# Who converts the gather indices: ScalarE ahead of time, or GpSimd in the place of a pause

## The chip, the cores and the metric

One core of a Trainium2 chip runs the whole program in one launch. The metric is the time of an execution on the device in microseconds (us); the kernel before has a median of 3063.61 us over three runs (3060.14 to 3072.32).

Five engines work beside each other, each in the order of its own program: TensorE (PE in the profile, with its weight loads as PEld), VectorE (DVE), ScalarE (ACT), GpSimd (POOL) and the queue of SyncE (SP), which here only issues transfers. They wait for each other by semaphores.

## The reference

A graph with 6250 nodes of 128 features and 200,000 edges, sorted by destination, goes through a layer norm with a ReLU and three layers of a GraphSAGE convolution. The output is the input plus the last layer's result.

```python
def _sage_conv(x, src, dst, Wl, bl, Wr):
    agg = jax.ops.segment_max(x[src], dst, num_segments=x.shape[0])
    agg = jnp.where(jnp.isfinite(agg), agg, 0.0)
    return agg @ Wl + bl + x @ Wr
...
h = jax.nn.leaky_relu(_sage_conv(h, src, dst, Wl, bl, Wr), 0.01)   # three times: 128 -> 256 -> 256 -> 128
```

What takes the time is `segment_max(x[src], dst)`: for each node the maximum, feature by feature, over the rows of all its neighbours. The neighbours are drawn at random, and some nodes have many more than others.

## The kernel before

Nodes stand in 50 tiles of up to 127. The kernel finds each node's maximum in two ways at once, and splits its edges between them.

The first way uses TensorE. Source nodes are taken two tiles at a time, in 25 pairs. For each pair, and for each block of destination nodes, an index says which source row (at most one in each half of the pair) the destination takes. ScalarE turns the indices into a one-hot matrix (`hot`, L1014 and L1016), TensorE multiplies the pair's features with it (L1033, into the PSUM tile `pg`, three buffers), and VectorE takes the maximum into `acc` (L1057). One such block is a step; the whole program is written out by hand as a row of steps over three layers.

The second way is for the edges that remain, and the change is in it. They stand in five lists (`Listed`, one object for each list and layer). A list has rows `q` of length `CAPS[k][q]`; each element of a row is one gather: GpSimd reads 128 indices, one for each partition, and issues an indirect DMA that fetches 128 rows of the layer's table from DRAM into a slot of the tile `g` (L1095). A layer has 503 gathers, the program 1509. Four gathers (eight in the first layer, whose rows are half as wide) fill one tile `g`, and there are 8 such tiles. When a tile is full, VectorE takes its maximum with the row's first tile (`maximum`, L1113), and at the row's end folds the slots together (`fold`, L1135); the result goes to DRAM (`store`), from where each node tile fetches it later (L1174).

The indices lie in SBUF as 16-bit numbers (`ell`, and `deep` for the first few gathers of a list), and the gather wants 32-bit ones. So up to four columns at a time (fewer at the end of a row) are converted into a small tile `let`, of which there are 14. `release` does that with a ScalarE activation (L1084). It is called for every gather, returns at once unless the gather is the first of its four, and stands in the program two steps ahead of that gather (`LEAD`).

Behind each gather stands a pause (L1102): GpSimd writes a tile of 128 x 300 that nobody reads. The pause is left out for the two gathers that follow a GpSimd subtraction in the second and third layer (`paused`, `SPARE`, L944); 1355 pauses are written in all.

`plan(t, rank, f)` puts a piece of work into step `t`; the ranks order the pieces within the step. At L1420 to L1423 each gather gets a step (`whens`, spread evenly over the layer), its `release` an earlier one and its `maximum` a later one (`delay`: 4 to 8 steps). GpSimd, like the others, works through its pieces in the order in which they were planned. Beside the gathers it has the fetches of L1174 and L1245, the subtractions of L944 for finished node tiles in the second and third layer, and, in the first layer, the scatters of L660 that build the lists; a small write of 128 x 1 stands ahead of each of those (L659).

Of the kernel before, what the change touches and what calls it, by code (L numbers as in the profile page):

```python
# [39 lines left out]
AF = mybir.ActivationFunctionType  # L40
# [31 lines left out]
FIRST = 24  # L72
# [5 lines left out]
def kernel(ctx: ExitStack, tc: tile.TileContext, x, src, dst,  # L78
                    Wl1, bl1, Wr1, Wl2, bl2, Wr2, Wl3, bl3, Wr3, out):
    nc = tc.nc  # L80
# [835 lines left out]
    for (f, k), s in best.items():  # L916
        n = len(LISTS[k]) * P
# [20 lines left out]
    paused = [0]  # L938
# [121 lines left out]
    class Listed:  # L1060
# [14 lines left out]

        def release(self, t):
            q, j = self.seq[t]
            if j % self.n:
                return
            assert here_now[0] >= listed_at[self.k]  # L1080
            n = min(self.n, self.long(q) - j)
            self.lets[q, j // self.n] = let = ring.tile([P, 4], I32, tag="let", name="let", bufs=14)
            of = ell[self.k][:, q, j : j + n] if q >= 0 else deep[self.k][:, j : j + n]
            nc.scalar.activation(let[:, :n], of, AF.Identity, scale=1.0)  # L1084

        def gather(self, t):
            q, j = self.seq[t]
            b, i = divmod(j, self.B)
            if i == 0:
                self.tiles[q, b] = ring.tile([P, self.B, self.F], F32, tag="g", name="g", bufs=RING)  # L1090
            if j % self.n == self.n - 1 or j == self.long(q) - 1:
                let = self.lets.pop((q, j // self.n))
            else:
                let = self.lets[q, j // self.n]
            nc.gpsimd.indirect_dma_start(  # L1095
                out=self.tiles[q, b][:, i, :], out_offset=None, in_=tables[self.layer],
                in_offset=bass.IndirectOffsetOnAxis(ap=let[:, j % self.n : j % self.n + 1], axis=0),
            )
            if paused[0]:
                paused[0] -= 1  # L1100
            else:
                nc.gpsimd.memset(gap_t, 0.0)  # L1102
# [184 lines left out]
    for layer in range(3):  # L1287
        begins.append(len(steps))
        for n in range(max(STARTS[layer]) + NG):
# [3 lines left out]
            of = {}  # L1293
# [16 lines left out]
    def plan(t, rank, f):  # L1310
        agenda.setdefault((t, rank), []).append(f)

    LET, TURN, MAXIMA, ROWS, REST, LINEAR, MERGE, SOONER, GATHER, FETCH = range(10)
    LEAD = 2
# [64 lines left out]
    def delay(layer, t):  # L1379
        return DELAY[layer] - (0 if layer else 4 if t < 92 else 2 if t < 150 else 0)  # L1380

    def heavy(layer, t):
        if layer:
            return WIDER if steps[t][3][3] is not None else 1.0
        return next((1.0 + w for w, until in zip(SLOWER, (58, 92, 150)) if t < until), 1.0)
# [17 lines left out]
    for layer in range(3):  # L1403
        b0, end = begins[layer], begins[layer + 1]
        lists_ = [Listed(layer, k) for k in range(NL)]
        whens = []
        for part, t0, t1 in ((lists_, max(b0 + 2, rows_at) if layer else EARLY, end - 1 - SOON),):
            total = [0.0]
            for t in range(t0, t1):
                total.append(total[-1] + heavy(layer, t))  # L1410
            n = sum(len(li.seq) for li in part)
            t = 0
            for i in range(n):
                while total[t + 1] <= total[-1] * i / n:
                    t += 1
                whens.append(t0 + t)
        done_at, i, at = [], 0, 0
        for k, li in enumerate(lists_):
            for t in range(len(li.seq)):
                plan(max(whens[i] - LEAD, 0) if layer or k or t >= FIRST else 0, LET, lambda li=li, t=t: li.release(t))  # L1420
                plan(whens[i], GATHER, lambda li=li, t=t: li.gather(t))
                at = max(at, whens[i] + (SOON if k == NL - 1 else delay(layer, whens[i])))
                plan(at, MAXIMA, lambda li=li, t=t: li.maximum(t))  # L1423
                last = t == len(li.seq) - 1
                to = at
                for n, f in enumerate(li.folds(t)):
                    if f == li.beside or n == 0 or (n and not last and li.seq[t][0] != 0):
                        to += 1
                    plan(to, MAXIMA, f)
                i += 1  # L1430
            done_at.append(to)
        gap = (2, 3, 3)[layer]
        def begin(key, make):
            def f():
                accs[key] = make()
                accs[key].fetch()
            return f

        def stages(ta, key, make, after=(3, 4, 5, 6)):
            plan(ta, FETCH, begin(key, make))  # L1440
            for d, rank, stage in (
                (after[0], MERGE, "merge"), (after[1], LINEAR, "linear"),
                (after[2], ROWS if after[2] > after[1] else SOONER, "rows"), (after[3], TURN, "turn"), (after[3], REST, "rest"),
            ):
                plan(ta + d, rank, lambda stage=stage: getattr(accs[key], stage)())

        def ready(k, i):
            return max(ends_at[layer, k], done_at[LISTED[GROUPS[k][i]][0]] + gap) + 1

        def node_of(k, i):  # L1450
            return (layer, k, "node", i), lambda layer=layer: Node(layer, k, i, accs[layer, k])

        joins = ready(VIRT, 0)
        key = (layer, "joined")

        def start(key=key, layer=layer):
            accs[key] = Joined(layer, accs[layer, VIRT])

        plan(joins, MAXIMA, start)
        for v in range(NV):  # L1460
            plan(joins + v, FETCH, lambda key=key, v=v: accs[key].fetch(v))
            plan(joins + 2 + v, MERGE, lambda key=key, v=v: accs[key].merge(v))
        for i in range(widths[layer] // P):
            plan(joins + 10, MERGE, lambda key=key, i=i: accs[key].scan(i))
        for v in range(NV):
            plan(joins + 11 + v, TURN, lambda key=key, v=v: accs[key].send(v))
        virtual_at = joins + 11 + NV + 2
        t, waiting = 0, [(layer, None, a) for a in range(VT)]
        for k, every in ((0, 1 if layer == 0 else 2), (1, 1 if layer == 0 else 2), (3, 1)):
            for i in range(len(GROUPS[k]) - 1, -1, -1):  # L1470
                t = max(t, ready(k, i))
                while waiting and t >= virtual_at:
                    a = waiting[0][2]
                    stages(t, waiting.pop(0), lambda layer=layer, a=a: Node(layer, None, a, None))
                    t += every
                stages(t, *node_of(k, i))
                t += every
        assert not waiting
        t0 = max(t, end, done_at[-1] + 1) + 1
        for j, i in enumerate(range(len(GROUPS[4]) - 1, -1, -1)):  # L1480
            stages(t0, *node_of(4, i), after=[d + j for d in (2, 3, 3, 4)])
        rows_at = t0 + 3 + len(GROUPS[4]) - 1
# [31 lines left out]
    for t in range(max(max(agenda)[0] + 1, len(steps) + 1)):  # L1514
# [10 lines left out]
        if t < len(steps):  # L1525
            st = steps[t]
            layer, k, _, _, _ = st
            if (layer, k) not in accs:
                i, o = ACC[k]
# [21 lines left out]
        def pair_at(t):  # L1551
            return steps[t][0], steps[t][4], steps[t][2]

        if here and (t == 0 or pair_at(t - 1) != pair_at(t)):
            i = at_pair[pair_at(t)] + 2
# [288 lines left out]
```

## Time and profile before

| | us |
|---|---|
| median of three runs | 3063.61 |
| the profiled execution | 3057.92 |
| its span, first to last instruction | 3056.0 |

The span has four parts: about 240 us in which the index tables are made, and then the three layers, whose gathers run from 241 to 1161, from 1224 to 2088 and from 2152 to 3005 us. In the second and third layer the first 450 us or so hold the list gathers with little else on GpSimd; after that the node tiles are finished beside the remaining gathers.

How to read the rows further down: a group of instructions has its line in the kernel, its engine, what it writes and reads (out<-in), the count behind an x, then busy time in us and the mean of one in ns. "Idle before" is the time in which the engine stood still right before these instructions, and the name behind the arrow is what ended most of it. In a timeline the same stands in brackets. "Issue" is time in which the engine waited for nothing that the profile shows.

### The profile page before, as it was taken

The page shows a single profiled execution, that of the slowest core. Times are in us where ns is not written, and L with a number is a line of the kernel's source. Part 1 is how long each engine was busy: PE and PEld are TensorE (multiplying, and loading weights), DVE is VectorE, ACT ScalarE, POOL GpSimd, SP SyncE. Part 2 cuts the span into 40 slices and gives each one's busy share as a digit, 9 for nine tenths or more (in the row PEclk, how much of TensorE's full clock was granted, in tenths as well). Part 3 has the DMA queues.
Part 4 walks back from the last instruction along what each step waited for, and adds up shares of the span by engine and source line. Part 5 has one row for each costly group of instructions (what it writes and reads, how often), then busy time and mean ns, then how long its engine had stood idle before and what let it go on. Part 6 is the DMA issues. An engine that isn't in the chain of part 4 may idle for free. (4 is left out here: it accounts for less than half of the span.)

```text
span 3056.0 us, 37265 instructions
## 1 busy us (share of the span) xinstructions
PE 2253.3 (74%) x9371; PEld 1679.8 (55%) x9371; DVE 2464.3 (81%) x4113; ACT 1551.2 (51%) x2734; POOL 2435.0 (80%) x3346
## 2 busy tenths in 40 slices
PE   1013545356665777998888879999899888878887
PEld 1012433344443545776666667776676666657665
DVE  6587966977896975898898988885798899988885
ACT  5204569466843766555455435555555545444342
POOL 6746888878888883888888887884788888887784
PEclk9996777677877999999999999999999999999998
DMA  9404434347754787555454547787555544546675
GB/s 257 130 6 129 125 98 120 105 122 226 225 156 150 226 243 254 163 167 180 134 162 152 160 148 237 248 265 263 160 170 164 159 138 151 173 148 183 196 220 161
DMA packets 301988, 525.13 MB, mean 172 GB/s; under 512 B 56769, under 2 KB 164439, under 8 KB 301125
## 3 DMA queue, kind: packets, MB, share of 16 engines
q1 hardware_dynamic: 205679, 293.70, 29.8%
q0 software_dynamic: 78016, 194.75, 23.2%
q10 hardware_dynamic: 18070, 34.20, 3.0%
q8 instruction: 79, 1.29, 0.2%
q14 instruction: 144, 1.18, 0.1%
HBM read 399.93 MB, written 122.51 MB: 171 GB/s over the span
## 5 line engine op out<-in xcount | busy, mean ns | idle before, releaser
L1033 PE MATMUL pg<-hot,pair_sb 128*128 128x512 f32 (+2 forms) x7500 | 1965.3, 411 | 422.0 <-DVE acc L1057 194.7
L1033 PEld LDWEIGHTS pg<-hot,pair_sb 128*128 128x128 f32 x7500 | 1412.4, 201 | 842.0 <-issue 291.4
L1095 POOL DMA_INDIRECT g<-table,let x1509 | 1531.1, 1015 | 346.0 <-issue 253.4
L1057 DVE TENSOR_TENSOR acc<-acc,pg 128x1024 f32<-128x1024 f32 (+5 forms) x1539 | 1543.2, 1024 | 238.5 <-PE pg L1033 130.8
L1016 ACT ACTIVATE hot<-idx_sb 128x1024 fp32r<-128x1024 uint8 (+3 forms) x975 | 839.5, 881 | 679.5 <-PE pg L1033 448.5
L1102 POOL MEMSET gap_t<- 128x300 f32 x1355 | 506.9, 374 | 0.6
L1014 ACT ACTIVATE hot<-idx_sb,last_b 128x1024 fp32r<-128x1024 int8 (+2 forms) x375 | 355.9, 949 | 33.8 <-PE pg L1033 24.7
L1113 DVE TENSOR_TENSOR g<-g 128x1024 f32<-128x1024 f32 (+7 forms) x211 | 209.6, 993 | 30.6 <-DMA g<-table,let 29.5
L1209 ACT ACTIVATE s<-z_p 127x256 f32<-127x256 f32 (+1 forms) x150 | 52.1, 347 | 329.0 <-PE z_p L1205 146.8
L1174 POOL DMA_INDIRECT agg<-best,end_i x141 | 142.5, 1011 | 54.2 <-PE aT_p L1190 22.7
L1135 DVE TENSOR_TENSOR g<-g 128x256 f32<-128x256 f32 (+2 forms) x365 | 174.8, 484 | 10.9 <-issue 6.5
L1203 PE MATMUL z_p<-wr,hT_in 128*128 128x256 f32 (+1 forms) x500 | 135.1, 387 | 0.7 <-DMA hT_in<-across 0.7
L1205 PE MATMUL z_p<-wl,mz 128*128 128x256 f32 (+1 forms) x500 | 121.0, 359 | 9.9 <-DVE mz L1196 7.7
L1004 DVE TENSOR_SCALAR idx_sb<-idx_sb,own_b 128x512 int32<-128x512 int32 (+4 forms) x125 | 74.3, 595 | 43.8 <-DMA idx_sb<-idx 35.5
L1203 PEld LDWEIGHTS z_p<-wr,hT_in 128*128 128x128 f32 x500 | 78.7, 199 | 42.4 <-issue 25.7
L1205 PEld LDWEIGHTS z_p<-wl,mz 128*128 128x128 f32 x500 | 88.4, 202 | 22.6 <-DVE mz L1196 10.2
L660 POOL DMA_INDIRECT picks<-picked,to_i x52 | 55.8, 1074 | 55.0 <-DVE rank_h L636 28.9
L1196 DVE TENSOR_TENSOR mz<-acc,aT_p 128x256 f32<-128x256 f32 (+1 forms) x141 | 52.1, 370 | 57.1 <-PE aT_p L1190 41.9
L793 DVE TENSOR_TENSOR acc<-acc 128x1300 int16<-128x1300 int16 (+6 forms) x120 | 62.2, 518 | 41.9 <-issue 20.0
L828 ACT CAST v<-lk_p 25x1024 uint8<-25x1024 bf16 (+4 forms) x15 | 10.8, 737 | 148.3 <-PE lk_p L826 134.7
L944 POOL TENSOR_TENSOR h<-s,h 127x256 f32<-127x256 f32 x50 | 37.9, 758 | 58.3 <-ACT h L1210 54.0
L1190 PE MATMUL aT_p<-ident,agg 128*128 128x128 f32 x250 | 57.1, 295 | 29.7 <-DMA agg<-best,end_i 17.1
(303 smaller groups left out, 1362.2 us busy)
## 6 DMA issues: line engine op xcount, KB each, us to landing
pair_sb<-pair SPq DMA_DIRECT2D x106, 512.0 KB
pair<-pr SPq DMA_DIRECT2D x100, 256.0 KB
g<-table,let POOLq DMA_INDIRECT x1509
pair_sb<-pair SPq DMA_DIRECT2D x85, 256.0 KB
idx_sb<-far SPq DMA_DIRECT2D x50, 384.0 KB
idx_sb<-far SPq DMA_DIRECT2D x50, 320.0 KB
idx_sb<-far SPq DMA_DIRECT2D x50, 304.0 KB
best<-g SPq DMA_DIRECT2D x104, 128.0 KB
```

Of the source, the lines that this page charges most:

```text
L1004: nc.vector.tensor_scalar(words, words, own_b.bitcast(I32)[:, 0:1], None, op0=OP.bitwise_xor)
L1014: nc.scalar.activation(hot[:, :w], far_b.bitcast(I8), AF.Relu, bias=last_b, scale=-1.0)
L1016: nc.scalar.activation(hot[:, :w], far_b, AF.Relu, bias=1.0, scale=-1.0)
L1033: nc.tensor.matmul(to, pr[:, s, i, kk * P : (kk + 1) * P], hot[:, o : o + bw], start=((alone or s == 0) and i == 0), stop=((alone or s == ...
L1057: nc.vector.tensor_max(to, to, of)
L1095: nc.gpsimd.indirect_dma_start(out=self.tiles[q, b][:, i, :], out_offset=None, in_=tables[self.layer], in_offset=bass.IndirectOffsetOnAxis ...
L1102: nc.gpsimd.memset(gap_t, 0.0)
L1113: nc.vector.tensor_max(base[:, : i + 1, :], base[:, : i + 1, :], g[:, : i + 1, :])
L1135: nc.vector.tensor_max(base[:, :h, :], base[:, :h, :], base[:, w - h : w, :])
L1174: nc.gpsimd.indirect_dma_start(out=self.agg[:, : self.F], out_offset=None, in_=of, in_offset=bass.IndirectOffsetOnAxis(ap=at, axis=0),)
L1203: nc.tensor.matmul(z_p, self.hT[:, i, :], wr[layer][:, i, :], start=False, stop=False)
L1205: nc.tensor.matmul(z_p, self.m[:, i, :], wl[layer][:, i, :], start=False, stop=(i == K - 1))
```

## The change

`release` is no longer planned. It converts with a GpSimd `tensor_copy` in place of the ScalarE activation, and `gather` calls it: for the first four columns of a list right ahead of the list's first gather, and from then on behind the first gather of each group of four, for the next group of the same list. Where such a copy is written, the pause behind that gather is not.

```diff
         def release(self, t):
             q, j = self.seq[t]
-            if j % self.n:
-                return
...
-            nc.scalar.activation(let[:, :n], of, AF.Identity, scale=1.0)
+            nc.gpsimd.tensor_copy(let[:, :n], of)
 
         def gather(self, t):
...
+            if (q, j // self.n) not in self.lets:
+                self.release(t)
...
             nc.gpsimd.indirect_dma_start(...)
-            if paused[0]:
+            after = t + min(self.n, self.long(q) - j)
+            if j % self.n == 0 and after < len(self.seq):
+                self.release(after)
+            elif paused[0]:
                 paused[0] -= 1
             else:
                 nc.gpsimd.memset(gap_t, 0.0)
...
-                plan(max(whens[i] - LEAD, 0) if layer or k or t >= FIRST else 0, LET, lambda li=li, t=t: li.release(t))
                 plan(whens[i], GATHER, lambda li=li, t=t: li.gather(t))
```

## Rows read from the trace of the kernel before

**Rows 1.** The page, busy time in us and share of the span, by engine

```profile
PE 2253.3 (74%) x9371; PEld 1679.8 (55%) x9371; DVE 2464.3 (81%) x4113; ACT 1551.2 (51%) x2734; POOL 2435.0 (80%) x3346
```

**Rows 2.** Groups on GpSimd, 1224 to 1700 us: busy, mean ns, idle before

```profile
L1095 POOL DMA_INDIRECT g<-table,let x310 | 312.0, 1006 | 78.3 <-issue 45.3 <-ACT hot L1016 26.5 <-DVE acc L1057 4.2
L1102 POOL MEMSET gap_t<- 128x300 f32 x309 | 113.2, 366 | 0.1
```

**Rows 3.** The same, 2152 to 2615 us

```profile
L1095 POOL DMA_INDIRECT g<-table,let x300 | 304.7, 1016 | 53.4 <-issue 46.0 <-DVE acc L1057 3.8 <-ACT hot L1016 1.6
L1102 POOL MEMSET gap_t<- 128x300 f32 x297 | 108.8, 366 | 0.1
```

**Rows 4.** Timeline, layer two's start: start, duration, instruction, idle before

```profile
1207.51 0.21 ACT L1084 ACTIVATE let<-deep 128x3 int32<-128x3 int16 x1
...
1220.11 0.32 SPq L1216 DMA_DIRECT2D table<-h  x1
...
1224.08 0.94 POOL L1095 DMA_INDIRECT g<-table,let  x1 [25.79 <-ACT hot L1016]
```

**Rows 5.** Waits, whole span: who for what, us in total, times, longest

```profile
DVE g L1113 <- DMA g<-table,let: 29.5, 17, 3.8
```

**Rows 6.** Waits of VectorE, 1224 to 1700 us

```profile
DVE acc L1057 <- PE pg L1033: 20.7, 34, 1.7
DVE g L1113 <- DMA g<-table,let: 13.4, 9, 3.4
```

**Rows 7.** Waits of VectorE, 2152 to 2615 us

```profile
DVE acc L1057 <- PE pg L1033: 22.0, 33, 4.4
DVE g L1113 <- DMA g<-table,let: 16.1, 8, 3.8
```

**Rows 8.** Timeline, one late gather in layer two

```profile
1517.18 1.23 DVE L1113 TENSOR_TENSOR g<-g 128x1024 f32<-128x1024 f32 x1 [3.42 <-DMA g<-table,let]
1517.41 1.82 POOL L1095 DMA_INDIRECT g<-table,let  x1 [0.17 <-issue]
...
1519.59 0.74 PE L1033 MATMUL pg<-hot,pair_sb 128*128 128x512 f32 x2 [3.46 <-DVE acc L1057]
```

**Rows 9.** Waits of GpSimd, 1700 to 2152 us

```profile
POOL h L944 <- ACT h L1210: 54.0, 19, 6.0
```

**Rows 10.** Busy time by stretch, line L1084 alone: us, ACT busy (count), clock, DMA

```profile
1224.00:1700.00 476.00, 16.75 (x94) 0.99 0.51 157
...
2152.00:2615.00 463.00, 16.55 (x91) 0.99 0.52 160
```

**Rows 11.** Timeline of GpSimd, a gather right behind a gather

```profile
1904.82 0.95 POOL L1095 DMA_INDIRECT g<-table,let  x1 [0.30 <-issue]
```

**Rows 12.** Timeline of GpSimd, scatters with a write of 128 x 1

```profile
184.43 0.12 POOL L659 MEMSET gap_t<- 128x1 f32 x1
184.74 0.97 POOL L660 DMA_INDIRECT picks<-picked,to_i  x1 [0.19 <-issue]
```

**Rows 13.** Line L944: count, duration ns min/median/max, first and last start us

```profile
L944 POOL TENSOR_TENSOR h<-s,h x50: 722/743/1135, 1825.1 to 2148.5; 127x256 f32<-127x256 f32 x50
L944 POOL TENSOR_TENSOR s<-s,h x50: 453/465/1232, 2755.9 to 3046.0; 127x128 f32<-127x128 f32 x50
```

**Rows 14.** Groups on GpSimd by form, whole span: the subtractions

```profile
L944 POOL TENSOR_TENSOR s<-s,h 127x128 f32<-127x128 f32 x50 | 25.2, 505 | 42.0 <-ACT h L1210 39.7 <-ACT let L1084 1.6 <-ACT s L1209 0.2
```

**Rows 15.** Timeline, a pause that starts during a fold

```profile
1503.44 1.22 DVE L1113 TENSOR_TENSOR g<-g 128x1024 f32<-128x1024 f32 x1
1503.69 0.36 POOL L1102 MEMSET gap_t<- 128x300 f32 x1
```

**Rows 16.** Groups on ScalarE and VectorE, 1224 to 1700 us

```profile
L1016 ACT ACTIVATE hot<-idx_sb 128x1024 fp32r<-128x1024 uint8 (+2 forms) x187 | 160.8, 876 | 202.3 <-PE pg L1033 157.9 <-issue 38.2 <-DMA idx_sb<-far 3.6
...
L1113 DVE TENSOR_TENSOR g<-g 128x1024 f32<-128x1024 f32 (+3 forms) x52 | 51.7, 994 | 14.2 <-DMA g<-table,let 13.4 <-issue 0.6
L1135 DVE TENSOR_TENSOR g<-g 128x512 f32<-128x512 f32 (+1 forms) x69 | 36.6, 531 | 5.6 <-issue 3.6 <-DMA g<-table,let 1.8
```

## The prediction

> **What bounds the kernel now.** I read the page first. It gives VectorE 81%, GpSimd 80% and TensorE 74% of the span [rows 1]: three engines close together, none of them full. Such shares are averages over unlike stages, so the groups by stretch come next, and there the reader is to add up GpSimd alone. From 1224 to 1700 us, the first part of the second layer, its 310 gathers take 312.0 us and the 309 pauses 113.2 us; the idle time ahead of gathers is 78.3 us [rows 2]. Of this, 25.8 us is one wait at the very start, for which see below [rows 4]. The rest is 78.3 - 25.8 = 52.5 us, that is 0.17 us ahead of each gather. 312.0 + 113.2 + 52.5 = 477.7 us, for a stretch of 476 us: GpSimd is never free. From 2152 to 2615 us it is the same: 304.7 + 108.8 + 53.4 = 466.9 us of 463 us [rows 3]. (The small excess is the instruction at the edges.) So in these two stretches GpSimd paces itself by gather, pause and the gap behind it, and waits for nobody.
>
> That alone does not make it the bound; somebody must wait for it. The table of waits shows that: VectorE waits 29.5 us, 17 times, for gathers ahead of the maximum of L1113 [rows 5], and of these 13.4 us, 9 times, fall into the first stretch and 16.1 us, 8 times, into the second [rows 6, 7]. That is all of them. The timeline shows one: VectorE stands 3.42 us until a gather has landed, and behind it TensorE stands 3.46 us because no PSUM buffer is free [rows 8]. So in these stretches, and in these only, GpSimd sets the pace. In the later part of each layer it waits itself, 54.0 us for ScalarE ahead of the subtractions from 1700 to 2152 us alone [rows 9], and no maximum waits for a gather. In the first layer none waits either. I expect no gain outside the two stretches.
>
> **The change part by part.** How many pauses go: each `let` conversion is one instruction today, and the rows have 94 in the first stretch and 91 in the second [rows 10]. In the first, three lists begin; those conversions stand ahead of a gather and replace nothing. In the second, two lists begin, and by the lists' lengths two of its conversions belong to gathers past 2615 us. That leaves 91 + 87 = 178 pauses replaced by a copy, and 5 copies that are extra.
>
> What a pause costs: 0.366 us [rows 2, 3] and the gap of 0.17 us to the next gather [rows 8], together 0.53 us. Had a gather followed directly, the gap would be 0.30 us [rows 11]. So a pause costs 0.23 us net, and this is the most that one replaced pause can give: 178 x 0.23 = 41 us. A small write between two scatters comes to the same: 0.12 us and then a gap of 0.19 us, together 0.31 us [rows 12].
>
> What a copy costs: the trace has no copy on GpSimd. The nearest operation that reads SBUF is the subtraction. It takes 0.453 us at least for 128 columns and 0.722 us for 256 [rows 13], so 0.0021 us a column and 0.184 us for none. It has two inputs, the copy has one, and at most four columns; I estimate 0.19 us. Its mean is 0.505 us where the least is 0.453 us [rows 13, 14], so 0.05 us is lost now and then to something; I add 0.03 us. The copy's slot is then 0.22 + 0.16 = 0.38 us, and a replaced pause gives 0.53 - 0.38 = 0.15 us. Both ends: the write of 128 x 1 makes it 0.31 us (gain 0.22 us, 39 us in all); a copy as dear as the mean subtraction of 128 columns takes 0.505 + 0.16 = 0.67 us (loss 0.14 us, 25 us in all). I take 0.15 us because four columns lie next to none.
>
> The sum on GpSimd: 178 x 0.15 = 26.7 us, less 5 x 0.38 = 1.9 us for the extra copies, is 25 us, half in each layer. Can it arrive? VectorE waits 29.5 us for gathers in the same stretches, so there is room for it; but it also waits 20.7 and 22.0 us for TensorE there [rows 6, 7], and a maximum that comes sooner will at times find the next product not ready. I let 21 us arrive.
>
> What ScalarE loses: 94 conversions, 16.75 us in the first stretch [rows 10]. It stands idle 202.3 us ahead of the one-hots there, mostly for TensorE [rows 16]; this work was covered and its end gives nothing. If that cover were not there, as where a one-hot is what TensorE waits for, it would be 0.18 us each time; I count none.
>
> What is moved: the conversions leave ScalarE's queue for GpSimd's. They are past no transfer: `release` issues none. New is that a gather waits for a copy on its own engine. Mostly that copy was issued a group earlier and the wait is over before it is reached. At the beginning of a list, and where a row ends with a group of one, the copy stands right ahead of its gather, and behind it all of GpSimd waits; this is in the slot of 0.38 us.
>
> The wait of 25.79 us at the second layer's start does not go. The profile names ScalarE, but the conversion was done at 1207.7 us; what came last before 1224.08 us is the store of the table's last rows, issued at 1220.11 us [rows 4]. The gather reads that table.
>
> The profiled execution took 3057.92 us, 5.7 us under the median of the runs. 3057.9 - 21 = 3036.9 us on its own terms; against the median, 3063.6 - 21 = 3042.6 us, which I forecast as 3042 us.
>
> **A rule against it.** The pause only writes, and a pause that starts 0.25 us into a fold of 1.22 us still takes 0.36 us [rows 15]. The copy reads SBUF, and the folds and maxima of L1113 and L1135 have both inputs in SBUF. In the first stretch these take 51.7 + 36.6 = 88.3 us [rows 16], 18.5% of it. If a copy that meets one stands until its end, it waits half of about 1 us in 18.5% of the cases: 0.09 us on the mean. The Trainium skill, "SBUF — State Buffer", section "Who interferes with whom", says just this: a VectorE instruction with two inputs in SBUF contends with a GpSimd instruction that reads SBUF, but not with one that only writes. On the pause the trace agrees with it; a GpSimd read that meets a fold in these stretches it does not have. By that rule the copy's slot is 0.38 + 0.09 = 0.47 us, and the sum is 178 x 0.06 - 5 x 0.47 = 8 us.
>
> **The rivals.**
> First, nothing that can be measured moves. The copy is about as dear as the pause, by the wait just worked out, or VectorE and TensorE, which wait for each other in the same stretches, take over at once. 8 us less: 3055 us. For it: the pair of waits of 20.7 and 22.0 us. Against it: VectorE's 29.5 us of waiting for gathers is real and is in these stretches only.
>
> Second, it gets slower: the copy is dearer than the pause. The place is GpSimd in the two stretches. The mechanism is one: the copy reads through what the folds use and stands there, and the gathers behind it come late by as much; since VectorE already waits for gathers there, all of it arrives. The point from which it decides is a mean copy of 0.37 us, the pause's own time. At 0.505 us it is 25 us and 5 x 0.67 = 3 us for the extra copies: 3092 us. For it: a subtraction took 1.135 or 1.232 us at worst [rows 13], and nothing in the trace shows a short GpSimd read beside folds. Against it: the mean subtraction is only 0.05 us above its least.
>
> Third, it gives more. The copy costs no more than the write of 128 x 1, and each replaced pause gives its 0.22 us: 39 us, less 2 us for the extra copies, is 37 us, or 3027 us. Against it: VectorE's waits for gathers sum to less.
>
> That the change does not do what it says can hardly be: counted in program order, 426 of the copies stand behind a gather and the pauses fall from 1355 to 933, four fewer than 426 because the pauses left out after a subtraction now fall on other gathers.
>
> **How the numbers follow.** What a measurement of this kernel tells from no change is about 0.5%, 15.3 us. The forecast case (12 to 30 us less) has 0.45, and a part of it, 0.08, ends under 15.3 us; no change has 0.27; slower has 0.18, of which 0.04 ends within 15.3 us; more has 0.10. Faster is 0.45 - 0.08 + 0.10 = 0.47, no change 0.27 + 0.08 + 0.04 = 0.39, slower 0.14. The range goes from 3016 us (47 us less: the third rival, and ScalarE's share with it) to 3078 us, which leaves out the dearest copies. The forecast case alone is 3033 to 3052 us.
>
> **What would show it.** In the changed profile the group of the copy on GpSimd should have x441 and a mean of 0.19 to 0.25 us, the pause x933. From one gather to the next with a copy between should be 1.33 us where it was 1.48 us. VectorE's wait for gathers at L1113 should fall from 29.5 us to under 15 us. The stretch of 310 gathers from the second layer's first should take about 465 us, and the third's 300 about 452 us. The first layer and the later halves should be as long as before. The forecast is wrong if the copy's mean is over 0.37 us, if VectorE's waits for gathers vanish and the stretches stay as long (then TensorE or VectorE binds), or if the time comes from the first layer or the layers' ends.

## The result

The changed kernel takes 3028.43 us (median of four runs, 3026.41 to 3031.41), the kernel before 3064.07 us beside it. The ratio is 0.9881, with an interval of 0.9851 to 0.991: 35.6 us, or 1.2%, faster. The forecast was 3042 us, 21 us faster. The profiled execution took 3027.8 us with a span of 3025.9 us, where that of before had 3056.0 us. Medians further down leave out two of the eight runs of one kernel, the later layers alone in the second group, which were in a slower state.

To see where the time went, each layer is measured from the start of its first gather to the start of its last (by the timelines; "the first 300" is the paced part that the forecast was about, up to the start of the 301st):

| us | before | after | difference | forecast |
|---|---|---|---|---|
| first layer | 919.1 | 897.7 | -21.4 | 0 |
| second layer | 861.3 | 856.0 | -5.3 | half of 21 |
| of it the first 300 gathers | 462.5 | 455.8 | -6.7 | |
| third layer | 852.3 | 840.8 | -11.5 | half of 21 |
| of it the first 300 gathers | 464.2 | 455.5 | -8.7 | |

The paced stretches gave 15.4 us, somewhat less than the 21 us forecast. The larger part came from the first layer, which was to give nothing.

### The profile after

The page, engines and groups (columns as in [rows 1, 2]); the line numbers have moved by up to three:

```profile
PE 2241.6 (74%) x9371; PEld 1668.8 (55%) x9371; DVE 2465.3 (81%) x4113; ACT 1511.4 (50%) x2293; POOL 2391.5 (79%) x3365
...
L1095 POOL DMA_INDIRECT g<-table,let x1509 | 1528.8, 1013 | 308.0 <-issue 253.9
...
L1105 POOL MEMSET gap_t<- 128x300 f32 x933 | 354.1, 380 | 0.3
...
L1116 DVE TENSOR_TENSOR g<-g 128x1024 f32<-128x1024 f32 (+7 forms) x211 | 209.8, 994 | 14.4 <-DMA g<-table,let 10.6
...
L1082 POOL CAST let<-ell 128x4 int32<-128x4 int16 (+3 forms) x426 | 114.6, 269 | 0.7
```

There are 933 pauses, as counted, and the mean copy takes 0.269 us, where 0.19 to 0.25 us were expected. VectorE waits 10.6 us for gathers in place of 29.5 us [rows 5]. The two stretches on GpSimd, from 1209 to 1665 us and from 2131 to 2587 us, the answer to [rows 2, 3]:

```profile
L1095 POOL DMA_INDIRECT g<-table,let x301 | 305.3, 1014 | 76.9 <-issue 47.5 <-DMA across<-hT 23.9 <-DVE acc L1057 2.6
L1105 POOL MEMSET gap_t<- 128x300 f32 x212 | 78.5, 370 | 0.1
L1082 POOL CAST let<-ell 128x4 int32<-128x4 int16 (+3 forms) x88 | 21.3, 242 | 0.1
...
L1095 POOL DMA_INDIRECT g<-table,let x301 | 302.1, 1004 | 53.6 <-issue 47.2 <-DMA table<-h 2.4 <-POOL let L1082 1.4
L1105 POOL MEMSET gap_t<- 128x300 f32 x210 | 76.8, 366 | 0.1
L1082 POOL CAST let<-ell 128x4 int32<-128x4 int16 (+3 forms) x88 | 26.3, 299 | 0.3
```

The wait of some 24 us at the second layer's start is still there, as forecast; the profile now puts it down to a transfer. GpSimd is still busy or in its gaps all the time, but who waits for it has changed. VectorE's waits in the same two windows (the answer to [rows 6, 7]; what, us in total, times, longest):

```profile
DVE acc L1057 <- PE pg L1033: 19.2, 29, 1.7
DVE g L1116 <- DMA g<-table,let: 10.6, 10, 1.8
...
DVE acc L1057 <- PE pg L1033: 25.5, 33, 4.4
DVE acc L1057 <- issue: 5.8, 12, 0.9
```

In the third layer no maximum waits for a gather any more: there GpSimd has stopped being the bound. Here are an ordinary copy and one that meets a maximum, on the timeline after (start, duration, instruction, idle before):

```profile
1270.59 0.37 POOL L1105 MEMSET gap_t<- 128x300 f32 x1
1271.13 1.02 POOL L1095 DMA_INDIRECT g<-table,let  x1 [0.17 <-issue]
1272.16 0.20 POOL L1082 CAST let<-ell 128x1 int32<-128x1 int16 x1
1272.51 0.97 POOL L1095 DMA_INDIRECT g<-table,let  x1 [0.16 <-issue]
...
2395.03 1.22 DVE L1116 TENSOR_TENSOR g<-g 128x1024 f32<-128x1024 f32 x1
2395.17 1.11 POOL L1082 CAST let<-ell 128x4 int32<-128x4 int16 x1
2396.16 0.68 DVE L1057 TENSOR_TENSOR acc<-acc,pg 128x512 f32<-128x512 f32 x1
```

From gather to gather with a copy between is 1.38 us here (1272.51 - 1271.13); over the two stretches the median is 1.33 us, as forecast, but the mean 1.46 us. The second copy starts 0.14 us into a maximum with both inputs in SBUF and ends when that ends. Of all 441 copies, 68 start inside such a maximum or fold and take 0.50 us on the mean; the other 373 take 0.22 us. Of the 53 among the 68 that take over 0.30 us, 51 end 0.04 to 0.05 us after the instruction that they met. This is the rule that the forecast weighed (the Trainium skill, "SBUF — State Buffer", section "Who interferes with whom"), and the trace agrees with it. The pause, which only writes, keeps its 0.37 us beside folds.

### The profile page after: what moved, and what is told of

Same layout as the page of the kernel before. It is cut to its first block, busy times and chain, and to the rows that moved or that the text cites. A ratio compares the mean times of both kernels' runs of the same rounds, so it can differ in the third digit from the quotient of the medians.

```text
span 3025.9 us, 36180 instructions
## 1 busy us (share of the span) xinstructions
PE 2241.6 (74%) x9371; PEld 1668.8 (55%) x9371; DVE 2465.3 (81%) x4113; ACT 1511.4 (50%) x2293; POOL 2391.5 (79%) x3365
## 3 DMA queue, kind: packets, MB, share of 16 engines
q1 hardware_dynamic: 205679, 293.70, 30.2%
q14 instruction: 136, 1.11, 0.1%
## 4 chain that ended last, share of the span: by engine, by line
PE 18%; POOL 15%; DVE 14%; issue 9%; DMA 3%; ACT 1%; SPq 1%; DVEq 0%; POOLq 0%; ACTq 0%; another core or an unknown queue 0%
PE pg L1033 14%; DVE acc L1057 11%; POOL g L1095 11%; POOL gap_t L1105 2%; PE z_p L1206 2%; PE z_p L1208 1%; DVE g L1116 1%; DMA g<-table,let 1%; POOL let L1082 1%; DMA pair_sb<-pair 1%; DVE g L1138 1%; DMA agg<-best,end_i 1%; POOL agg L1177 1%; PE aT_p L1193 0%; POOL h L944 0%
## 5 line engine op out<-in xcount | busy, mean ns | idle before, releaser
L1057 DVE TENSOR_TENSOR acc<-acc,pg 128x1024 f32<-128x1024 f32 (+5 forms) x1539 | 1544.2, 1025 | 259.7 <-PE pg L1033 143.6
L1016 ACT ACTIVATE hot<-idx_sb 128x1024 fp32r<-128x1024 uint8 (+3 forms) x975 | 834.9, 881 | 701.9 <-PE pg L1033 455.8
L1105 POOL MEMSET gap_t<- 128x300 f32 x933 | 354.1, 380 | 0.3
L1116 DVE TENSOR_TENSOR g<-g 128x1024 f32<-128x1024 f32 (+7 forms) x211 | 209.8, 994 | 14.4 <-DMA g<-table,let 10.6
L1082 POOL CAST let<-ell 128x4 int32<-128x4 int16 (+3 forms) x426 | 114.6, 269 | 0.7
L944 POOL TENSOR_TENSOR h<-s,h 127x256 f32<-127x256 f32 x50 | 38.0, 761 | 64.4 <-ACT h L1213 61.0
```

The lines of the kernel that those rows point to most:

```text
L1016: nc.scalar.activation(hot[:, :w], far_b, AF.Relu, bias=1.0, scale=-1.0)
L1057: nc.vector.tensor_max(to, to, of)
L1082: nc.gpsimd.tensor_copy(let[:, :n], of)
L1116: nc.vector.tensor_max(base[:, : i + 1, :], base[:, : i + 1, :], g[:, : i + 1, :])
```

## The experiments

There are three groups of runs, each on a chip of its own. Times are compared within a group only; the kernel before took 3066.89, 3090.49 and 3090.38 us in them. The diffs are shortened to the lines that matter. The expectations name theories by letters: A is GpSimd's time (copy for pause), B is ScalarE's part in the first layer, as a wait of GpSimd for the conversion (B1) or as load on ScalarE (B2), L is late signals between engines, which take back some of what closer gathers gain.

### First group: which part, and where (before 3066.89 us)

**The first layer alone.** ScalarE keeps converting in the second and third layer, with the pauses there as before.

```diff
-                plan(max(whens[i] - LEAD, 0) if ... else 0, LET, ... li.release(t))
+                if layer:
+                    plan(max(whens[i] - LEAD, 0) if ... else 0, LET, ... li.release(t))
```

> The change in the first layer alone; the other two layers are as before. In the changed kernel the gathers of the first layer took 21 us less from the first to the last (919 to 898 us), where I had forecast nothing; the two later layers gave some 16 us together. Theory A (GpSimd's time): the 142 replaced pauses of the first layer shorten its work, 142 x 0.10 us = 14 us or a little more, and the time is 3064 - 14 to 21, about 3046 us. Theory B (ScalarE's queue): gathers of the first layer waited 30.9 us for conversions on ScalarE, and the one-hots stood behind them; the same 3043 to 3050 us. Theory C (chance): the first layer's length depends on how the engines happen to meet, the 21 us don't belong to the change, and the time is 3064 us within 10.

3046.35 us, ratio 0.9921 (0.9891 to 0.995): 20.5 us of the gain is in the first layer, which is 902.5 us long. The later layers are as before (861.1 and 855.7 us).

**Copies that nobody reads.** ScalarE converts as before and is read; GpSimd does the same copies into another tile, in the same places, with the same pauses left out.

```diff
+            nc.gpsimd.tensor_copy(unread[:, :n], of)      # behind the first gather of four
             nc.scalar.activation(let[:, :n], of, AF.Identity, scale=1.0)
```

> ScalarE converts as before and the gathers read what it wrote. GpSimd makes the same copies in the same places and leaves out the same pauses as in the changed kernel, but into a tile that nobody reads. So GpSimd's program has the length of the changed kernel's and ScalarE's that of before. Theory A: all of the gain stays, 3028 us. Theory B: only the part of the paced stretches stays, about 16 us: 3048 us. Theory C: between, with the first layer anywhere.

3046.25 us, 0.9929 (0.99 to 0.9957). GpSimd's part is all here, and the later layers gain as in the change (855.4 and 839.7 us); the first does not (923.7 us). So the two gains are separate: GpSimd's time in the paced stretches, and something that goes with ScalarE's conversions in the first layer.

**The pauses dropped, nothing in their place.**

```diff
+            if j % self.n == 0 and after < len(self.seq):
+                pass
-            if paused[0]:
+            elif paused[0]:
```

> ScalarE converts as before; behind the gathers where the changed kernel has a copy there is nothing at all, neither copy nor pause. Each place gives 0.53 - 0.30 = 0.23 us of GpSimd where the copy gave 0.53 - 0.45 = 0.08 to 0.10 us. Theory A: the paced stretches give 178 x 0.23 = 40 us if TensorE and VectorE let them, and the first layer gives 142 x 0.23 = 33 us: 2991 us. Theory B: the first layer is as before, the stretches give up to 40 us: 3024 us.

3060.79 us, 0.9987 (0.9969 to 1.0006): no gain, where both theories had one. The paced parts take 451.6 and 456.5 us, together no shorter than with the unread copies (453.2 and 453.4 us). VectorE's waits there, all that is over 1 us:

```profile
DVE acc L1058 <- PE pg L1034: 29.5, 38, 2.9
DVE acc L1058 <- remote: 5.7, 4, 2.7
DVE acc L1058 <- issue: 5.0, 10, 0.9
DVE acc L1058 <- ACT acc L1056: 1.6, 1, 1.6
...
DVE acc L1058 <- PE pg L1034: 30.0, 37, 4.3
DVE acc L1058 <- remote: 9.7, 5, 3.6
DVE acc L1058 <- issue: 6.4, 13, 0.9
```

No wait for gathers is left (29.5 us before); VectorE waits for TensorE, 59.5 us, and 15.4 us have no releaser on this core that the profile can name ("remote"). The stretches have a floor of 452 to 456 us that GpSimd's own time does not set. The first layer is longer (928.6 us): there GpSimd waits 45.9 us for ScalarE's conversions (30.9 us before).

**Copy and pause.** GpSimd copies, and all 1355 pauses stay.

```diff
-            elif paused[0]:
+            if paused[0]:
```

> GpSimd copies as in the changed kernel and the gathers read it, but the pause behind those gathers is kept, behind the copy. ScalarE is relieved as in the changed kernel; GpSimd's slot there is about 0.27 us longer than before. Theory A: the paced stretches lose 178 x 0.27 = 48 us and the first layer up to 142 x 0.27 = 38 us: 3110 to 3150 us. Theory B: the first layer keeps its 21 us and the stretches lose 48 us: 3091 us.

3108.12 us, 1.0144 (1.0116 to 1.0172). VectorE's waits for gathers in the two stretches:

```profile
DVE g L1137 <- DMA g<-table,let: 24.1, 12, 4.0
...
DVE g L1137 <- DMA g<-table,let: 28.8, 15, 5.4
```

These are 52.9 us, and 300 gathers take 478 and 477 us. With 29.5 us before, 10.6 us after and none in the run without pauses, for 463, 456 and 454 us on the mean, theory A holds in the stretches of this chip and the first one, down to the floor.

### Second group: ScalarE's part (before 3090.49 us)

**ScalarE works again.** The changed kernel, with ScalarE converting into a tile that nobody reads.

```diff
+                plan(max(whens[i] - LEAD, 0) if ... else 0, LET, ... li.unread_act(t))
                 plan(whens[i], GATHER, lambda li=li, t=t: li.gather(t))
```

> The changed kernel, and ScalarE converts too, in the places where it did before, into a tile that nobody reads. ScalarE's load is that of before (a few waits less), but no gather waits for it. Two theories for the first layer's 21 us, both with ScalarE in them. B1 (the wait): GpSimd stood for conversions that stood behind other work in ScalarE's queue (13.6 us in the first layer before, beside one wait at its start); now it waits for its own copy. Then the gain stays: 3028 to 3033 us. B2 (the load): the one-hots behind the conversions come sooner. Then 15 to 20 us are given back: 3045 us.

3102.63 us, 1.0059 (1.0032 to 1.0085). The changed kernel is not in this group, so what was given back is read in the next.

**Converted earlier.** The kernel before, its conversions in the first layer six steps ahead of the gather and not two.

```diff
-                plan(max(whens[i] - LEAD, 0) if ...
+                plan(max(whens[i] - (LEAD if layer else 6), 0) if ...
```

> The kernel before, with the first layer's conversions planned six steps ahead of their gathers where it was two; ScalarE does them, all pauses stay. B1: the waits of gathers for conversions go and a good part of the first layer's 21 us comes: 3046 to 3056 us. B2: nothing changes, 3066 us.

3068.12 us, 0.9936 (0.9914 to 0.9958): 22 us faster, with the same number of conversions on ScalarE, and a first layer of 904.4 us.

**A shorter pause.** The changed kernel with `PAUSE = 150` in place of 300.

```diff
-PAUSE = 300
+PAUSE = 150
```

> The changed kernel with pauses of 150 columns in place of 300, some 0.12 us less for each of 933. With the pause dropped at every fourth gather the two paced stretches came down to 452 to 457 us from 462 and 464, no further than with the copy (456, 455), and VectorE waited no more for gathers there. So theory A' (VectorE and TensorE have taken over): the stretches stay at 450 to 455 us, and the time is 3020 to 3030 us. Theory A (GpSimd still paces): 440 gathers with a pause in the stretches give 440 x 0.7 x 0.12 = 37 us more: 2991 us.

3371.06 us, 1.0915 (1.0878 to 1.0952): 9% slower than the kernel before, which neither theory foresaw. Groups and waits of the whole span:

```profile
L1058 DVE TENSOR_TENSOR acc<-acc,pg 128x1024 f32<-128x1024 f32 (+5 forms) x1539 | 1549.4, 1026 | 570.8 <-PE pg L1034 251.4
...
L1126 POOL MEMSET gap_t<- 128x150 f32 x933 | 233.4, 250 | 0.9 <-remote 0.4
...
PEld pg L1034 <- issue: 487.5, 310, 25.4
DVE acc L1058 <- remote: 207.8, 62, 12.6
ACT hot L1017 <- remote: 116.1, 31, 7.6
```

The pause went from 0.38 to 0.25 us, gathers no longer hold VectorE, and yet VectorE stands 570.8 us ahead of L1058 (259.7 us in the changed kernel), 207.8 us of it "remote". One such place on its timeline:

```profile
1604.90 1.65 PE L1034 MATMUL pg<-hot,pair_sb 128*128 128x384 f32 x8 [1.53 <-issue]
...
1611.73 0.97 POOL L1111 DMA_INDIRECT g<-table,let  x1 [0.16 <-issue]
1611.93 1.22 DVE L1058 TENSOR_TENSOR acc<-acc,pg 128x1024 f32<-128x1024 f32 x1 [6.86 <-remote]
...
1613.30 1.19 PE L1034 MATMUL pg<-hot,pair_sb 128*128 128x256 f32 x4 [6.75 <-issue]
```

The last matmul recorded ends near 1606.5 us; VectorE starts its next maximum over 5 us later, while GpSimd issues one gather after another at 1.37 us. The page counts 9371 matmuls, as in the other kernels. Why the signal comes late stays open.

**The later layers alone.** ScalarE converts in the first layer as before.

```diff
+                if not layer:
+                    plan(max(whens[i] - LEAD, 0) if ... else 0, LET, ... li.release(t))
```

> The change in the second and third layer alone. The two paced stretches give 7 to 9 us each and the rest nothing: 3067 - 16 = 3051 us. If the gains of the first and the later layers add, this and the kernel with the first layer alone (20.5 us less) sum to the change (some 36 us less).

3098.64 us, 1.0047 (1.0013 to 1.0081): without the first layer's part the change is not faster on this chip.

### Third group: the same with the change beside it (before 3090.38 us)

**The change again,** without any edit.

> The changed kernel once more, so that the next two can be compared with it on one chip. In the last call the kernel before took 3090 us, where it had taken 3064 and 3067 us, and both halves that were tried there, ScalarE's work put back and the change in the later layers alone, came out 0.5% slower than before. Theory T (the gain holds wherever it is measured): the ratio to before is 0.988 again. Theory L (lateness): in the kernel with the shorter pause VectorE waited for products whose matmuls had long been issued, 208 us at L1057 against 13 us in the changed kernel; the closer the gathers follow each other, the more of this, and how much differs by chip. Then on a chip where before takes 3090 us the change gains little or nothing, and on one where it takes 3065 us it gains its 1.2%.

3079.20 us, 0.9965 (0.9946 to 0.9985): 11 us, a third of what it gave at first: theory T falls.

**ScalarE works again**, the kernel of the second group.

> As e5_scalar_work_back, beside the changed kernel. B1 (the first layer's gain was GpSimd's wait for conversions): within 5 us of the changed kernel. B2 (it was ScalarE's load): 15 to 20 us over it.

3093.82 us, 1.0018 (0.9993 to 1.0042): 14.6 us over the changed kernel, though no gather waits for these conversions. B1 alone falls.

**The later layers alone**, once more.

> As e8_later_layers_only, beside the changed kernel. If the gains of the layers add as in the first call (20.5 us for the first layer alone), it is 20 us over the changed kernel.

3096.68 us, 1.0025 (0.9999 to 1.0052), 17.5 us over the changed kernel: the first layer's part again.

**A longer pause.** The changed kernel with `PAUSE = 360`.

```diff
-PAUSE = 300
+PAUSE = 360
```

> The changed kernel with pauses of 360 columns in place of 300, 0.05 us more for each of 933. Theory A (GpSimd's time paces the stretches): some 430 pauses lie there, 430 x 0.05 = 21 us, of which a part is taken up by others as with the copy and the pause together (14 us of 24): 10 to 20 us over the changed kernel. Theory L: VectorE's late products get fewer and the time is the same as the changed kernel's or less.

3072.23 us, 0.9946 (0.9921 to 0.9971). By GpSimd's time alone it should be slower than the changed kernel; it is 7 us under it, with intervals that overlap. On this chip longer pauses cost nothing, which speaks for L. VectorE's waits at the maximum of a step with "remote" as releaser were 30.2 us in the change again and 12.5 us here. The evidence is thin: the two profiled executions took 3067.72 us (the change again, the second shortest of twelve) and 3072.93 us (here), so these traces don't show the gain itself.

### What the first layer's gain is

Neither B1 nor B2 fits all of these runs: converting earlier gains with the load unchanged, and converting for nobody loses with no wait at all. The traces hold a third cause. Here is ScalarE in the kernel before, and what stands behind it (timeline; an engine's name with q is its queue issuing a transfer):

```profile
410.18 1.04 ACT L1016 ACTIVATE hot<-idx_sb 128x1024 fp32r<-128x1024 uint8 x1
...
423.14 0.97 POOL L660 DMA_INDIRECT picks<-picked,to_i  x1 [0.19 <-issue]
...
425.25 0.32 SPq L671 DMA_DIRECT2D ell<-picks  x1
...
427.32 0.33 ACTq L1501 DMA_DIRECT2D far<-idx_sb  x1
...
427.69 3.20 ACT L783 ACTIVATE acc<-rows_w,keys 128x520 int16<-128x520 int16 x5 [16.46 <-DMA ell<-picks]
...
430.92 1.37 DVE L793 TENSOR_TENSOR acc<-acc 128x1300 int16<-128x1300 int16 x2 [13.38 <-issue]
...
431.98 0.79 PE L1033 MATMUL pg<-hot,pair_sb 128*128 128x512 f32 x1 [19.50 <-issue]
```

GpSimd writes the third list's rows by scatters until 424 us; only then may SyncE load the list (`ell<-picks`, L671). ScalarE has nothing to do with that list here. Its next piece is to store an index tile (`far`, L1501, in ScalarE's own queue), and it stands 16.46 us until the list has been loaded, VectorE and TensorE behind it. The changed kernel has the same store and the same load:

```profile
409.88 0.33 ACTq L1503 DMA_DIRECT2D far<-idx_sb  x1
409.98 0.71 ACT L783 ACTIVATE acc<-rows_w,keys 128x520 int16<-128x520 int16 x1
...
425.95 0.97 POOL L660 DMA_INDIRECT picks<-picked,to_i  x1 [0.19 <-issue]
...
428.08 0.32 SPq L671 DMA_DIRECT2D ell<-picks  x1
```

Here nothing stands still. What the store waits for is in the built programs. The transfers that SyncE and ScalarE issue are numbered in one list and take eight semaphores in turn (101 to 108 in the traces; the gathers and scatters of GpSimd have eight others, 109 to 116), and a transfer waits until the one that had its semaphore last is done. (The Trainium skill, "DMA: Bandwidth & Descriptors", section "Anatomy of one DMA — SWDGE (gpsimd) path", says that a transfer's wait for a semaphore is made by the engine that issues it, not by the DMA engines. The trace agrees: ScalarE does no work for these 16.46 us.) From the list's load on, with the eight numbered 0 to 7:

```
before: ell 6, deep 7, deep 0, deep 1, deep 2, best 3, idx 4, pair 5, far 6
after:  ell 6, deep 7, deep 0, deep 1, deep 2, best 3, idx 4, far 5, pair 6
```

In the kernel before the store is the eighth transfer behind the load and has its semaphore; in the changed one it has moved one place ahead. The records of the traces bear it out in every kernel of the table below: the load has semaphore 107, and the store waits for 107 in each of the seven with a wait, and for 106 in each of the six without. Apart from conversions and pauses, each engine's own order is the same in both. The delay reaches the gathers through GpSimd: its scatters for the next list, the fourth, wait for VectorE's ranks. The first fence has this wait in the kernel before, between 593 and 708 us, the second after, between 592 and 698 us:

```profile
POOL picks L660 <- DVE rank_f L637: 13.9, 1, 13.9
```
```profile
POOL picks L660 <- DVE rank_f L637: 5.7, 1, 5.7
```

GpSimd waits there in both, so where these scatters start is set by the ranks and not by GpSimd. They part the first layer into pieces (by the starts of gathers and scatters):

| us | before | after | difference |
|---|---|---|---|
| first gather to the fourth list's scatters | 378.2 | 364.9 | -13.3 |
| from there to the 471st gather | 472.4 | 467.3 | -5.1 |
| from there to the last gather | 68.6 | 65.5 | -3.1 |

The first piece goes with the store: in the seven kernels with its wait the scatters start 376.6 to 381.2 us behind the first gather, in the run without pauses too (378.7 us), and in four without it at 364.1 to 368.1 us. (In the other two, the longer pause and copy and pause, GpSimd itself comes late, at 370.1 and 376.4 us, and waits only 1.6 and 0.6 us.) The second piece is GpSimd's own time once more: in the kernel before it has 4.7 us of waits over 0.45 us there, and in the change 74 copies of 19.6 us stand for 72 pauses of 26.4 us. In the third, a gather of the kernel before waits 2.1 us for its conversion.

ScalarE's wait for the list's load at this place, from each kernel's trace, beside the length of its first layer:

| kernel | wait, us | first layer, us |
|---|---|---|
| before | 16.5 | 919.1 |
| copies unread; pause dropped | 14.0; 12.3 | 923.7; 928.6 |
| ScalarE works again, twice | 13.5; 13.4 | 918.7; 932.3 |
| later layers alone, twice | 13.7; 15.9 | 929.8; 931.0 |
| after; change again | none | 897.7; 909.2 |
| first layer alone | none | 902.5 |
| converted earlier | none | 904.4 |
| longer pause | none | 909.3 |
| copy and pause | none | 926.7 |

The chips differ here too: later layers alone has the first layer of the kernel before and takes some 11 us more than that did on the first chip. But on the first group's chip and the one of the result (897.7 and 902.5 against 919.1 to 928.6 us) as on the other two (904.4 to 909.3 against 918.7 to 932.3 us), all but one fall into two groups, and the kernel converted earlier, where ScalarE converts as much as before, is among those without the wait. The exception has the wait in two other places: 9.4 us for a `deep` load between 400 and 470 us and 14.6 us for the fifth list's load after 880 us, and it has longer slots on GpSimd besides. The shorter pause is left out, since its whole time is upset. No run parts the store from the load and does nothing else, so this cause is read from the traces of runs with other aims, and not tested by itself.

## Why the prediction was right, and where it was not

**The bound.** Right: GpSimd paced the two stretches, VectorE waited for it there, and its waits for gathers fell from 29.5 to 10.6 us (under 15 us was forecast). The stretches shrank less than forecast: 471 us for 310 gathers of the second layer (465 us forecast) and 455.5 us for 300 of the third (452 us).

**What a replaced pause gives.** 0.15 us was forecast, with a slot of 0.38 us for the copy. The ordinary copy was sized rightly (0.20 us and a gap of 0.16 us in the timeline); the term that was too small is the 0.03 us added for what is lost now and then. The mean over the two stretches is 48.4 us for 180 copies, 0.27 us, since those that meet a fold or maximum stand until its end. With the gap of 0.17 us the slot is 0.44 us, and with 0.54 us for a pause (0.37 us and its gap) a replaced one gives 0.10 us: 178 x 0.10 - 5 x 0.44 = 15.6 us, against 15.4 us measured in the first 300 gathers of the two layers. That they agree so closely is luck: in the run with the first layer alone, on another chip and with later layers as before, these parts took 459.7 and 465.7 us, 2.8 us less and 1.5 us more than in the kernel before. The rule against the change was right, and its wait nearly so: by it a copy loses 0.09 us on the mean, and it lost 0.27 - 0.20 = 0.07 us. Its sum of 8 us was too low, the forecast's 25 us too high.

**What of it arrives.** The forecast took 4 us off for TensorE. On the first chip all of the 15 us arrived, within that spread. The run without pauses shows that little more was to be had: the floor is 452 to 456 us.

**What is moved.** Here a step failed: "They are past no transfer: `release` issues none", and with it "I expect no gain outside the two stretches". The conversions issue no transfer, but taking them out of ScalarE's program moved a store one place in the list of transfers, and so away from a semaphore that was held for 16.5 us. By the traces this accounts for 13.3 of the 21.4 us that the profile's first layer gave; the run with the first layer alone is 20.5 us faster. The other step that failed is "In the first layer none waits either" as a reason for no gain there: no maximum waits, but from the fourth list's scatters on GpSimd hardly waits itself, and its shorter slots gave 5.1 us there as they did in the stretches. The prediction names this as a sign of being wrong, "if the time comes from the first layer", and more than half of it did. That ScalarE's own time counts for nothing was right where it was said, in the stretches: the unread copies gain there as much as the change does.

**The sum.** 3042 us against 3028.43 us, too high by 14 us: outside the forecast case's own 3033 to 3052 us, and inside the whole range only because that reaches down for the third rival. That the total lies there at all is partly luck: the stretches alone gave 15.4 us, and the larger part came from the layer that was forecast at nothing. The profiled spans are 30.1 us apart: 15.4 us from the paced stretches (21 forecast), 21.4 us from the first layer, 1.4 us from the later halves, less 8.1 us outside the layers' gathers, of which 4.2 us are a later first gather (245.1 us, before 240.9 us).

**The rivals.** The first (nothing moves) had the wait at folds in it, which came, but TensorE and VectorE took over only at the end of the gain. The second needed a mean copy of 0.37 us; it was 0.27 us. The third has the right time (3027 us) for a wrong reason: the copies cost more than the write of 128 x 1, and the rest came from the first layer.

**How far it holds.** On the chips of the second and third group the kernel before takes 3090 us; on the third's the change gives 11 us, not 36. The first layer's part is there as well (14.6 and 17.5 us over the changed kernel without it), so the change in the later layers brings nothing there: the later layers alone are 8 and 6 us slower than before, the 6 us with an interval that reaches zero. In the second group's traces the two paced parts take 462.5 and 459.1 us with the change in them and 460.5 and 464.6 us without it (converted earlier), 3.5 us less in all. Why is open. More waits for "remote" signals, 30.2 us at L1057 in the change again and 12.6 us after, may point to the same effect as in the shorter pause; no run shows it.

## What to carry to other kernels

Add up an engine that paces a stretch by its whole slot, instruction and gap, and give a small instruction that reads SBUF the waits of those copies that meet a two-input instruction of VectorE. Before saying that an edit moves no transfer, list which transfers share a semaphore before and after it: a store that inherits the semaphore of a load held by other work stops its whole engine (16.5 us here), and an edit that moved conversions alone made or parted such a pair. An engine whose results nobody is seen to wait for can still set the length of a stretch, if it hardly waits itself. A pause can be dear and still be needed, and its length is worth a run in both directions.

## What the hardware showed that was not expected

- Halving the columns of the pause between gathers (0.38 to 0.25 us) made the kernel 9% slower than the one before; other engines' signals came late (207.8 us of VectorE's waits with no releaser named), and the granted clock over the span was 0.876 where the other kernels of that group had 0.908 to 0.914.
- A GpSimd copy of four columns takes 0.20 us, and up to 1.11 us when it starts in a maximum with two inputs in SBUF.
- A store on ScalarE's queue stood 16.46 us, and ScalarE with it, for a load of SyncE's queue that had the same semaphore (107) and nothing else to do with it.
- The same change gave 1.2% on one chip and 0.35% on another, whose kernel before is 0.9% slower.
